# Layer 0 of a four-layer graph network: the transposes of a block's sums and of the next queries moved to the end of a round of scores

## The chip, the cores and the metric

The kernel runs on one core of a Trainium2 chip. The time is the device time of one execution in microseconds (us); the number to predict is the median over several executions. A profile of one further execution gives the busy time of each engine: PE (TensorE matmuls, with PEld for its weight loads), DVE (VectorE), ACT (ScalarE), POOL (GpSimd) and SP (SyncE, which here issues DMAs).

## The reference, cut to what matters

Four graph layers follow one another on x (4096 x 64) with one adjacency matrix adj (4096 x 4096, zeros and ones, about one entry in a thousand set). The change is in layer 0:

```python
h = jnp.maximum(_layernorm(x, axis=-1), 0.0)
h = lorentz_linear(h, W, b, scale)
q = lorentz_linear(h, Wq, bq, scale_q)
k = lorentz_linear(h, Wk, bk, scale_k)
att = 2.0 + 2.0 * (qm @ k.T)          # qm is q with its first column negated
att = adj * jax.nn.sigmoid(att / att_scale + att_bias)
support = att @ h
x = x + support / denorm              # a length of each row of support
```

Each layer begins with `_layernorm` and a maximum with zero. Layers 1 to 3 use the same adj: a weighted count over each row's last neighbours, a plain product, and a mean over neighbours.

## The kernel before, in words

**Tiling.** The 4096 rows whose sums are formed are cut into eight blocks of 512 (`NIB` blocks, numbered 7 down to 0, in this order). The 4096 rows that are summed over are cut into 32 tiles of 128, taken two at a time as a group g (`NG` = 16 groups). One step of layer 0 is one pair (block, g): `scores` (L910) makes two fp32 matmuls, each with half of PE's rows, into a PSUM tile `ps` of 128 x 1024; `sigmoids` (L926) applies the sigmoid on ACT, into `ps` itself or, for the first step of a round of four, into an SBUF tile `att`; `masked` (L932) multiplies by the mask on DVE into `att` (L940); `gather` (L942) multiplies `att` with the rows `fb` on PE and adds into the block's accumulator `acc`, each of its two matmuls in half of PE's columns (L947). Three `ps` tiles are used in turn: a score needs the tile of three scores before. The one of a round's first score is free when its sigmoid is done, the others when DVE's product is.

**Rounds.** The main loop (L1047) takes steps in rounds, of four as a rule, and in the first block of the loop (block 6) in rounds of 4, 4, 3 and 3. A round issues its scores one after the other and then the products of the round before. Each engine works through its own queue in the order in which the program emits the instructions. Before the loop, a planned part (`first_rows_and_block`) has done block 7 and two steps of block 6.

**Work between the rounds.** After each step of a round, `on()` (L1037) advances two things by one turn. `step()` advances a list of generators, each of which runs to its next `yield`; a job pushed with a number lets the jobs behind it go on only after that many turns. `rows0` (L878) is such a job, pushed when a block's accumulator is full: transposes of the block's sums (`turned`, L231, 128 x 128, four of them, into the PSUM tile `pt`), a copy of them on ACT (L237), an addition on POOL (L239), a square on ACT (L888), the sums `inn` on DVE (L891 to L894), an inverse square root (`rsqrt`: a first value on DVE, L256, then twelve small POOL instructions, L260 to L263), two POOL instructions of 256 elements (L896, L897), then `norm` for layer 1: `st` on DVE (L271), `xc` on POOL (L275), a square on ACT (L278), `va` on DVE (L281), a second `rsqrt` on POOL, `xc` on DVE (L297), and `split` (L245 on POOL, L248 on DVE). The second thing is `queries` (L870): two transposes of the next block's queries (L855, into the PSUM tile `pq`), and four copies of them on ACT into `qt` (L865). `pt` and `pq` share one PSUM buffer.

**What else is in the stage.** Every step issues one mask load on POOL's queue as long as there are any left (L175). From block 5 on, five steps of eight do a `check` (L342): a load of 256 KB on SP's queue and one DVE instruction on it (L356), which looks for entries of adj that are neither zero nor one. `count_constants` (L819) is a job of its own, in block 6, with POOL and DVE instructions. After layer 0, `chunks_counted` (L1139) runs 256 matmuls over the masks, with `step()` now and then, and the layer 1 products follow.

Before the change the transposes come where the generators' own counts of `yield` put them: those of `pt` two turns after `rows0` is begun, and those of `pq` six turns after `queries`.

Of the kernel before, what the change touches and what calls it, by code (L numbers as in the profile page):

```python
# [48 lines left out]
def kernel(  # L49
# [77 lines left out]
    def bc(col, r):  # L127

        return col.unsqueeze(2).to_broadcast([P, r, D])

    def over_rows(v, r):
        return v.unsqueeze(1).to_broadcast([P, r, v.shape[-1]])

    def model(general):
# [4 lines left out]
        def pool(name, bufs, on=stack, **kw):  # L139
            return on.enter_context(tc.tile_pool(name=name + sfx, bufs=bufs, **kw))  # L140
# [9 lines left out]
        def rows_in(gr):  # L150
# [10 lines left out]
        todo = [  # L161
            (ib, g) for ib in order0 for g in (first_cols if ib == order0[0] else range(NG))
        ]
        masks = {}

        def get_mask(mp, ib):

            masks[ib] = mp.tile([P, NT, IB], FP8, name=f"mask{ib}{sfx}")
# [30 lines left out]
        def rows_tile(name, tag, on=epi, bufs=1, dtype=F32):  # L199
            return on.tile([P, CI, D], dtype, tag=name, name=f"{name}{tag}{sfx}", bufs=bufs)  # L200

        def small(name, tag, on=epi, n=CI):
            return on.tile([P, n], F32, tag=name, name=f"{name}{tag}{sfx}")
# [14 lines left out]
        def turned(asb, b, tag, adding=False):  # L218


            shape = (P, CI, D if adding else P)
            if b is None:
                pt = pm.tile(list(shape), F32, tag="pr", name=f"pt{tag}{sfx}")
            else:
                pt = bank(b, f"pt{tag}", shape)
            for c in range(CI):
                part = asb[:, c * P : (c + 1) * P]
                if adding:
                    nc.tensor.matmul(pt[:, c, :], part, fold, start=True, stop=True)
                else:  # L230
                    nc.tensor.transpose(pt[:, c, :], part, ident)  # L231
            return pt

        def halves_added(to, asb, pt):

            v = asb.rearrange("p (c i) -> p c i", c=CI)
            nc.scalar.copy(v, pt)  # L237
            yield
            nc.gpsimd.tensor_tensor(to, v[:, :, 0:D], v[:, :, D:P], ALU.add)  # L239
            yield  # L240

        def split(h, s2, rows):


            nc.gpsimd.tensor_scalar(s2[:, rows, 0, :], h, 1.0 / STEP, None, ALU.mult)  # L245
            yield
            yield
            nc.vector.scalar_tensor_tensor(  # L248
                s2[:, rows, 1, :], s2[:, rows, 0, :], -STEP, h, ALU.mult, ALU.add
            )  # L250

        def rsqrt(v, tag, on=epi, n=CI, key=""):


            y, a = (small(f"rs_{a}{key}", tag, on, n) for a in "ya")
            nc.vector.tensor_scalar(  # L256
                y.bitcast(I32), v.bitcast(I32), -0.5, 1597463007.0, ALU.mult, ALU.add
            )
            for _ in range(3):
                nc.gpsimd.tensor_tensor(a, y, y, ALU.mult)  # L260
                nc.gpsimd.tensor_tensor(a, a, v, ALU.mult)
                nc.gpsimd.tensor_scalar(a, a, -0.5, 1.5, ALU.mult, ALU.add)
                nc.gpsimd.tensor_tensor(y, y, a, ALU.mult)  # L263
            return y
# [38 lines left out]
        def push(job, lag):  # L303

            jobs.append([job, lag])
# [20 lines left out]
        def drain():  # L326
            while jobs:
                step()

        def block(ib):  # L330
            return slice(ib * CI, (ib + 1) * CI)
# [514 lines left out]

        stream0 = pool("stream0", 1, l0) if general else None
        spare, turn = [], [0]
        qts = {}

        def queries_turned(ib, pt):

            for k in range(CI // 2):
                c = ib * CI + 2 * k
                nc.tensor.transpose(  # L855
                    pt[:, k, :], q_sb[:, c : c + 2, :].rearrange("p c d -> p (c d)"), ident
                )

        def queries_laid(ib, pt):

            qt = work.tile([P, IB], F32, tag="qt", name=f"qt_{ib}{sfx}", bufs=2)
            to = qt.rearrange("p (k c i) -> p k c i", k=CI // 2, c=2)
            for c in range(2):
                for s in range(2):
                    nc.scalar.copy(  # L865
                        to[s * D : (s + 1) * D, :, c, :], pt[c * D : (c + 1) * D, 0 : CI // 2, :]
                    )
            qts[ib] = qt

        def queries(ib):  # L870
            for _ in range(6):
                yield
            pt = pm.tile([P, CI, P], F32, tag="pr", name=f"pq_{ib}{sfx}")
            queries_turned(ib, pt)
            yield
            queries_laid(ib, pt)

        def rows0(ib, asb):  # L878
            tag = f"0_{ib}"
            rows = block(ib)  # L880
            yield
            yield
            pt = turned(asb, None, tag)
            yield
            sup = rows_tile("sup", tag)
            yield from halves_added(sup, asb, pt)
            sq = rows_tile("sq", tag)
            nc.scalar.activation(sq, sup, AF.Square)  # L888
            yield
            inn = small("inn", tag)  # L890
            nc.vector.tensor_reduce(inn, sq, AX.X, ALU.add)  # L891
            nc.vector.scalar_tensor_tensor(inn, sq[:, :, 0], -2.0, inn, ALU.mult, ALU.add)
            nc.vector.scalar_tensor_tensor(inn, inn, -1.0, inn, ALU.mult, ALU.max)
            nc.vector.tensor_scalar(inn, inn, 1e-8, None, ALU.max)  # L894
            rs = rsqrt(inn, tag)
            nc.gpsimd.tensor_tensor(sup, sup, bc(rs, CI), ALU.mult)  # L896
            nc.gpsimd.tensor_tensor(x_sb[:, rows, :], x_sb[:, rows, :], sup, ALU.add)  # L897
            yield
            yield
            yield  # L900
            yield
            h = yield from norm(rows, None, tag, False)
            yield from split(h, s2a, rows)
            ready.setdefault(1, set()).add(ib)

            nc.gpsimd.tensor_tensor(
                x_sb[:, rows, :], x_sb[:, rows, :], over_rows(bias1, CI), ALU.add
            )
# [116 lines left out]
        with tc.manual_schedule():  # L1025
            acc, late = first_rows_and_block()
            push(rows0(order0[0], evacuated(order0[0], acc, 0)), 10)
            pro_stack.close()
            mp1 = pool("mask_b", 1, side="right")
            for ib in order0[EARLY:]:  # L1030
                get_mask(mp1, ib)
            spare.append(pool("pp1", 1, l0, space=PSUM))
            if not general:
                push(count_constants(), 1)
            asking = iter(())

            def on():  # L1037
                step()
                next(asking, None)

            sizes = [2] * 8 if general else [4] * 4
            first = [2] * 7 if general else [4, 4, 3, 3]
            sizes = first + (NIB - 2) * sizes + [0]
            k, done = NG + 2, NG
            for size in sizes:  # L1047
                now = []
                for ib, g in todo[k : k + size]:
                    ps = scores(ib, g)  # L1050

                    if size == 4 and not now:
                        att = frm = sigmoids(ps, att_tile(ib, g))
                    else:
                        frm, att = sigmoids(ps), att_tile(ib, g)
                    masked(ib, g, frm, att)
                    now.append((ib, g, att))
                    load_masks(1)
                    k += 1
                    if k > 2 * NG and k % 8 in (0, 2, 4, 5, 7):  # L1060
                        check()
                    on()
                for ib, g, att in late:
                    at = done % NG
                    if at == 0:
                        acc = pa0.tile([P, IB], F32, tag="pa", name=f"acc0_{ib}{sfx}")
                        if ib > 0:
                            asking = queries(ib - 1)
                    gather(acc, fb, g, att, at)
                    if at == NG - 1:  # L1070
                        push(rows0(ib, evacuated(ib, acc, 0)), 10)
                    done += 1
                late = now
            if len(checks) % 2:
                check()
            if general:
                drain()
# [440 lines left out]
    with tc.If(any_odd[0] > 0):  # L1518
        model(True)
# [49 lines left out]
```

## Time and profile before

| | |
|---|---|
| median of three executions | 605.93 us (605.20 to 606.10) |
| the profiled execution | 605.98 us, of which the span 604.2 us |
| PE busy | 563.6 us (93%), 3012 matmuls |
| DVE busy | 484.8 us (80%) |
| ACT busy | 335.6 us (56%) |
| POOL busy | 238.1 us (39%) |
| scores, L916 on PE | 512 matmuls, 127.5 us busy |
| products, L947 on PE | 512 matmuls, 117.6 us busy |
| granted clock of PE, mean | 0.99 |

The span runs from the first to the last instruction of the profile, and 1.8 us of the profiled execution lie around it. In the views below, a line of a timeline has the start in us from the span's start, the length of the run of instructions in us, the engine, the line of the program, the operation, what is written and read, the shape and the number of instructions; in brackets the engine's idle time ahead of it, and what ended it. A line of the chain that ended last has a start, a length and a piece of work. A line of the table by stretch has the stretch, its length, the busy time and number of instructions of PE, PEld, DVE, ACT and POOL in it, PE's granted clock, the mean busy share of the DMA engines and the GB/s. Ends of matmuls are modelled, so starts are the safer numbers.

### The profile page before, as it was taken

What the parts mean: (1) busy time and instruction counts of PE and PEld (TensorE: products, weight loads), DVE (VectorE), ACT (ScalarE), POOL (GpSimd) and SP (SyncE); (2) the same over time, 40 slices, a digit from 0 to 9 for tenths busy, and PEclk for the clock granted to TensorE, in tenths of its full rate; (3) what the DMA queues carried; (4) which work ended last, traced back from release to release, by engine and by line L of the source; (5) the groups of instructions that cost most, each with busy time, mean ns of one, the idle gap of its engine ahead of it and who ended that gap; (6) DMA issues with size and microseconds to landing.
All of it is one profiled execution on the core that took longest, in us unless ns stands there. A gap on an engine that the chain in (4) does not pass through costs nothing.

```text
span 604.2 us, 8998 instructions
## 1 busy us (share of the span) xinstructions
PE 563.6 (93%) x3012; PEld 235.5 (39%) x3012; DVE 484.8 (80%) x941; ACT 335.6 (56%) x541; POOL 238.1 (39%) x459
## 2 busy tenths in 40 slices
PE   0777999899999999899999999999998999999995
PEld 0563333233333333233343343343443545454553
DVE  5769766699999999799966878879888669987753
ACT  1557657667666666676626677767766013441221
POOL 8422401585767675754335400100010305452252
PEclk9996999999999999999999999999999999999999
DMA  9992932679999999992262555555455476445921
GB/s 139 143 105 23 101 30 18 61 100 158 151 161 158 151 157 162 139 149 88 71 247 102 168 183 168 160 193 165 157 199 181 151 267 208 151 164 186 316 91 41
DMA packets 43015, 87.02 MB, mean 144 GB/s; under 512 B 5136, under 2 KB 22032, under 8 KB 42960
## 3 DMA queue, kind: packets, MB, share of 16 engines
q1 hardware_dynamic: 23808, 68.40, 34.4%
q0 software_dynamic: 18720, 17.57, 31.1%
q10 hardware_dynamic: 432, 0.40, 0.3%
q8 instruction: 25, 0.41, 0.3%
q14 instruction: 30, 0.25, 0.1%
HBM read 135.63 MB, written 1.05 MB: 226 GB/s over the span
## 4 chain that ended last, share of the span: by engine, by line
PE 86%; DVE 4%; ACT 4%; issue 2%; POOL 2%; DMA 2%; ACTq 0%; DVEq 0%; POOLq 0%
PE acc L1321 18%; PE ps L916 18%; PE acc L947 17%; PE acc L1249 9%; PE cnt L1211 9%; PE cnt L1221 3%; PE many L1144 2%; PE pt L231 2%; PE ps_h L624 1%; DVE att L940 1%; PE pr L1124 1%; DMA vec<-vecs_dram 1%; PE ps_q L624 1%; PE pn L1398 1%; ACT tq L767 1%
## 5 line engine op out<-in xcount | busy, mean ns | idle before, releaser
L916 PE MATMUL ps<-qt,kt 64*128 64x512 f32 x512 | 127.5, 623 | 3.5 <-DVE att L940 3.4
L356 DVE SCALAR_TENSOR_TENSOR ckw<-ckw 128x1024 f32<-128x1024 f32 x98 | 124.9, 1283 | 5.9 <-DMA ckw<-adjt_dram 5.7
L947 PE MATMUL acc<-att,fb 128*64 128x512 f32 x512 | 117.6, 599 | 0.0
L1237 ACT ACTIVATE w<-cnt 128x512 int16<-128x512 f32 x176 | 93.1, 597 | 42.8 <-PE cnt L1221 42.5
L940 DVE TENSOR_TENSOR att<-ps,mask 128x1024 f32<-128x1024 f32 x84 | 101.1, 1219 | 9.8 <-ACT ps L929 8.9
L929 ACT ACTIVATE ps<-ps,att_c,att_a 128x1024 f32<-128x1024 f32 x84 | 95.7, 1173 | 10.0 <-PE ps L916 7.0
L929 ACT ACTIVATE att<-ps,att_c,att_a 128x1024 f32<-128x1024 f32 x44 | 52.5, 1204 | 56.1 <-PE ps L916 53.1
L175 POOL DMA_DIRECT2D mask<-adjt_dram x128 | 70.3, 563 | 21.3 <-DMA mask<-adjt_dram 19.1
L916 PEld LDWEIGHTS ps<-qt,kt 64*128 64x128 f32 x512 | 44.7, 188 | 76.1 <-DVE att L940 21.5
L1235 DVE TENSOR_SCALAR w<-cnt 128x512 int16<-128x512 f32 x80 | 53.7, 687 | 23.1 <-PE cnt L1221 22.7
L940 DVE TENSOR_TENSOR att<-att,mask 128x1024 f32<-128x1024 f32 x44 | 56.3, 1292 | 18.2 <-ACT att L929 17.6
L1211 PE MATMUL cnt<-mask,after 128*128 128x512 fp8e4 x256 | 66.3, 379 | 2.0 <-DVE w L1235 1.5
L1249 PE MATMUL acc<-w,s2a 128*128 128x512 bf16 x256 | 66.5, 381 | 0.1
L947 PEld LDWEIGHTS acc<-att,fb 128*64 128x64 f32 x512 | 33.6, 136 | 79.2 <-issue 75.4
L275 POOL TENSOR_TENSOR xc<-x_sb,st 128x256 f32<-128x256 f32 x24 | 19.1, 795 | 108.4 <-DVE st L272 54.9
L1321 PE MATMUL acc<-mask,s2a 128*128 128x512 fp8e4 x256 | 57.8, 379 | 0.0
L1321 PE MATMUL acc<-mask,s2b 128*128 128x512 fp8e4 x256 | 57.7, 379 | 0.0
L260 POOL TENSOR_TENSOR rs_a<-rs_y 128x4 f32<-128x4 f32 x48 | 16.8, 350 | 81.6 <-DVE rs_y L256 72.3
L356 DVE SCALAR_TENSOR_TENSOR ck<-ck 128x512 f32<-128x512 f32 x60 | 44.9, 749 | 0.3 <-DMA ck<-adjt_dram 0.3
L1211 PEld LDWEIGHTS <-after 128*128 128x128 bf16 x256 | 24.8, 99 | 30.9 <-issue 3.5
L1321 PEld LDWEIGHTS <-s2b 128*128 128x128 f16 x256 | 25.0, 98 | 27.6 <-issue 0.8
L1321 PEld LDWEIGHTS <-s2a 128*128 128x128 f16 x256 | 24.6, 98 | 27.3
(194 smaller groups left out, 582.4 us busy)
## 6 DMA issues: line engine op xcount, KB each, us to landing
ckw<-adjt_dram SPq DMA_DIRECT2D x98, 512.0 KB, 3.5
mask<-adjt_dram POOLq DMA_DIRECT2D x128, 128.0 KB, 9.0
ck<-adjt_dram SPq DMA_DIRECT2D x60, 256.0 KB, 5.1
x_sb<-x_dram SPq DMA_DIRECT2D x4, 256.0 KB, 7.8
out_dram<-y POOLq DMA_DIRECT2D x6, 128.0 KB, 2.2
out_dram<-y ACTq DMA_DIRECT2D x2, 128.0 KB, 2.2
w_sb<-wts_dram SPq DMA_DIRECT2D x2, 80.0 KB, 7.6
vec<-vecs_dram ACTq DMA_DIRECT2D x1, 130.5 KB, 6.3
```

What stands on the lines that cost most here:

```text
L175: nc.gpsimd.dma_start(out=masks[ib][:, g * CG : (g + 1) * CG, :], in_=adjt[ib, g])
L275: nc.gpsimd.tensor_tensor(xc, xr, bc(st, CI), ALU.add)
L356: nc.vector.scalar_tensor_tensor(at, at, 0.0, at, ALU.not_equal, ALU.not_equal, accum_out=odd[:, k : k + 1])
L916: nc.tensor.matmul(ps[:, c, :], kt[half, g, :], qts[ib][half, :], start=True, stop=True)
L929: nc.scalar.activation(to, ps, AF.Sigmoid, bias=att_c, scale=att_a)
L940: nc.vector.tensor_tensor(att, frm, mask, ALU.mult)
L947: nc.tensor.matmul(acc[c * D : (c + 1) * D, :], lhs[:, t, :], rhs[:, c, :], start=(at == 0), stop=(at == NG - 1), skip_group_check=True,)
L1211: nc.tensor.matmul(cnt, after, masks[ib][:, t, :], start=True, stop=True, skip_group_check=True)
L1235: nc.vector.tensor_scalar(w, cnt, 0.0, None, ALU.max)
L1237: nc.scalar.activation(w, cnt, AF.Relu)
L1249: nc.tensor.matmul(accs[ib], both(s2a, t), w, start=(t == NT - 1), stop=False, skip_group_check=True,)
L1321: nc.tensor.matmul(acc, both(s2, t), masks[ib][:, t, :], start=(t == 0), stop=(t == NT - 1), skip_group_check=True,)
```

## The change

A flag, `edge`, tells the generators whether the step just emitted is the last of its round of scores. `rows0` now waits at least one turn and then until the flag is set before it transposes; `queries` waits three turns and then until the flag is set. After the loop the flag is left set. The instructions themselves are the same; what follows the transposes in the two generators follows by as many turns as before.

```diff
+        edge = [False]
         qts = {}
@@ def queries(ib):
-            for _ in range(6):
+            for _ in range(3):
+                yield
+            while not edge[0]:
                 yield
             pt = pm.tile([P, CI, P], F32, tag="pr", name=f"pq_{ib}{sfx}")
             queries_turned(ib, pt)
@@ def rows0(ib, asb):
             yield
-            yield
+            while not edge[0]:
+                yield
             pt = turned(asb, None, tag)
@@ the main loop
-                for ib, g in todo[k : k + size]:
+                for n, (ib, g) in enumerate(todo[k : k + size]):
+                    edge[0] = n == size - 1
                     ps = scores(ib, g)
@@ after the main loop
                 late = now
+            edge[0] = True
             if len(checks) % 2:
```

In the order in which the changed program emits its instructions, the transposes of `pt` of blocks 7 to 1 stand after the round's last score, where they stood before it; those of `pq` of blocks 4 to 0 stand after the last score of a block's third round, where they stood before the last score of its fourth. The later steps of `rows0` stand one step later, and ACT's copies of the queries stand between the sigmoids 12 and 13 of an ordinary block, where they stood after sigmoid 15.

## The prediction

> **What bounds the kernel now.** I read the busy shares first (PE 93%, DVE 80%, ACT 56%, POOL 39%), then the chain that ended last (86% of it on PE), then the stage of the change: a table by block of layer 0, the timelines of the engines inside it, and the chain around the two places where PE stands still. A "block" below runs from one block's first `acc` product to the next one's; the six full ones and the last, shorter one are, with PE, PEld, DVE, ACT and POOL busy in each:
>
> ```profile
> 95.03:129.54 34.51, 32.64 (x144) 11.00 (x142) 26.32 (x46) 23.75 (x27) 18.28 (x48) 1.00 0.51 50
> 129.54:159.77 30.23, 30.23 (x136) 10.41 (x134) 28.47 (x50) 21.01 (x24) 18.11 (x42) 1.00 1.00 154
> 220.67:253.37 32.70, 31.11 (x136) 10.26 (x138) 28.81 (x49) 21.22 (x25) 21.24 (x48) 1.00 0.99 150
> 253.37:283.71 30.34, 30.34 (x136) 10.44 (x138) 28.84 (x49) 21.00 (x24) 16.88 (x38) 1.00 0.68 128
> ```
>
> To see: in an ordinary block PE has no idle time, but DVE has only 1.5 to 1.8 us of it. The two blocks left out are like the second (30.40 and 30.50). So PE sets the end, with DVE close behind. PE idles in the first block (1.87 us) and in one later one (1.59 us).
>
> The timeline of PE prices the thing that is moved:
>
> ```profile
> 104.11 2.85 PE L916 MATMUL ps<-qt,kt 64*128 64x512 f32 x12
> 106.89 0.44 PE L855 MATMUL pq<-ident,s2a 128*128 128x128 f32 x2
> 107.26 3.65 PE L947 MATMUL acc<-att,fb 128*64 128x512 f32 x16
> ...
> 155.35 2.85 PE L916 MATMUL ps<-qt,kt 64*128 64x512 f32 x12
> 158.13 0.66 PE L231 MATMUL pt<-ident,asb 128*128 128x128 f32 x4
> 158.71 1.13 PE L916 MATMUL ps<-qt,kt 64*128 64x512 f32 x4
> 159.77 3.65 PE L947 MATMUL acc<-att,fb 128*64 128x512 f32 x16
> 163.36 3.70 PE L916 MATMUL ps<-qt,kt 64*128 64x512 f32 x16
> 166.99 3.65 PE L947 MATMUL acc<-att,fb 128*64 128x512 f32 x16
> ```
>
> From start to start: four undivided scores take 166.99-163.36 = 3.63, four products 3.59. Three scores take 2.78, the 0.85 left for a further one being its pure length. But the fourth score behind the transposes takes 159.77-158.71 = 1.06. So a switch of the form of matmul costs about 0.2 us. The first query transposes of layer 0 happen to lie at the end of a round already (106.89): they take 0.37 us up to the products, as they do between scores (143.12 to 143.49), and the products behind them keep their 3.58. Moving transposes to the end of a round thus saves one switch of 0.2 us, with nothing paid for it on PE.
>
> **What the skill says.** The Trainium skill, TensorEngine Tiling (Array Packing), Key Properties: changing the tiling mode drains TensorE. The scores use half the rows, the products half the columns, the transposes all: the trace agrees, with 0.2 us. SBUF — State Buffer, Who interferes with whom: a DVE instruction with two SBUF inputs and a GpSimd instruction that reads SBUF block each other. The trace agrees: a 0.19 us step of `rsqrt` (L262) took 1.04 us at 158.01, under a mask product from SBUF. PSUM — Partial Sum Buffer, Engine vs sequencer instructions: the queues of ScalarE, VectorE and GpSimd are strictly in order; the trace shows ACT's square L278 holding up sigmoids that were ready (from 241.80 to 244.48, below).
>
> **The change on PE.** Twelve groups of transposes move from before a round's last score to behind it: the sums `pt` of blocks 7 to 1 (seven), and the queries `pq` of blocks 4 to 0 (five), which also go from the fourth round to the third. 12 x 0.20 = 2.4 us saved. `pq` of block 5 goes from one round's end to another's: nothing. `pt` of block 0 moves earlier inside the counting products L1144: nothing, as PE runs through there with or without it (0.58 us either way).
>
> **The change in the first block.** Its two holes, by the chain that ended last and PE's timeline:
>
> ```profile
> 113.12 0.36 ACT qt L865
> ...
> 114.66 1.19 ACT ps L929
> ...
> 115.87 1.22 DVE att L940
> ...
> 118.62 1.22 DVE att L940
> ...
> 119.90 1.99 PE L916 MATMUL ps<-qt,kt 64*128 64x512 f32 x8 [1.57 <-DVE att L940]
> ```
>
> The four query copies (1.51 us) sit between sigmoids 13 and 14, and everything behind them is late; three PSUM tiles take turns, so the third score of the next round waits for DVE's product 15. Now they sit behind sigmoid 10. By hand, from the start X of that round (before: 110.84): sigmoid 13 at +1.18, product 13 on DVE +2.39, `st` 0.55, product 14 at +4.08, the constants 1.61 us, product 15 from +6.83 to +8.05. The score needs it 0.26 earlier than its own start (0.06 to see it, 0.2 for weights), so it starts at +8.31; undisturbed it would at 2.78+2.73+0.2+1.71 = +7.42. The hole is 0.89, where before it is 1.57+0.2 = 1.77: 0.88 saved. The second hole (0.30 at 126.84, and the 0.2 to start again, and a little before it: 0.58) came from product 3, queued on DVE behind `xc` L297, which waited for POOL. That step is now behind product 3: 0.58 saved. Together 1.5 us.
>
> **What is late next.** Two new waits, in each ordinary block. The rows for them, of DVE, POOL and ACT, around the block start at 148.13:
>
> ```profile
> 140.63 0.17 DVE L256 TENSOR_SCALAR rs_y<-inn 128x4 int32<-128x4 int32 x1
> ...
> 147.20 2.73 POOL L175 DMA_DIRECT2D mask<-adjt_dram  x5
> 149.90 0.68 POOL L275 TENSOR_TENSOR xc<-x_sb,st 128x256 f32<-128x256 f32 x1
> ...
> 145.89 1.52 ACT L865 COPY qt<-pq 64x256 f32<-64x256 f32 x4
> ...
> 150.61 0.42 ACT L278 ACTIVATE sq<-xc 128x256 f32<-128x256 f32 x1
> ```
>
> (a) The query copies, today after sigmoid 15 where ACT is idle, come between sigmoids 12 and 13. From the start of that round: sigmoid 12 at +1.17, the copies +2.28 to +3.80, sigmoid 13 ends +4.97, product 13 on DVE +5.01, product 14 +6.15, a check 0.61, product 15 from +7.90 to +9.12. The next block's scores start at 3.63+3.59 = +7.22 (no transposes in this round now), its third score at +9.13, and needs +9.38. Late by 0.25; with the checks at their mean (0.75, not 0.68 us) 0.3. Five blocks: 1.5 us. What shrinks the round is itself what uncovers this: today it has 0.57 more.
>
> (b) `inn`, the sum of squares, moves behind product 11 and a check: it ends about 9.7 us after its round starts (2.41 to the first product, four of 1.14, `split`'s 0.37, two checks of 0.61, its own 1.15), where before it was 140.80-133.12 = 7.7. From there to `xc` takes POOL 149.90-140.80 = 9.1 us: twelve steps of `rsqrt`, two of 256 elements, and five mask DMAs of 0.55 that are issued in between. So `xc` starts at 18.8, and the next block at 7.59+7.22 = 14.8: `xc` is 4.0 into it (before 1.8). ACT's square then starts at +4.7 and holds back sigmoid 2, queued behind it, to +5.05, with its end +6.22; product 2 on DVE +6.26, `va` 0.76, product 3 +8.16 to +9.38. Round two's third score would start at +9.38 and needs +9.64: late by 0.26. The mean check instead of the short one, three times, makes it 0.45; with POOL's steps blocked once more by a product from SBUF (0.85) it is up to 1.3; with POOL less blocked than before, nothing. I take 0.45. It meets four blocks, since in the last one no mask is left to issue: 1.8 us.
>
> No DMA changes in number; the mask issues keep their places between POOL's other work but for one that goes ahead of the first `halves_added`, and SP's order is the same. The checks' loads follow the checks. Behind layer 0 nothing is due: block 0's normed rows are wanted only by the last products of the first counting group.
>
> **Sum.** -2.4 -1.5 +1.5 +1.8 = -0.6 us. Against the profiled execution, 605.98 us with a span of 604.2: 605.4, span 603.6. The median is 605.93, so 605.3. A difference of 0.2% (1.2 us) is about what a measurement of this kernel can tell from none.
>
> **Rivals.** (1) Full gain: the two waits stay covered, because POOL is blocked less in the place where its steps now run (one check less beside them), and (a) is absorbed: -2.4-1.5 = -3.9, 602.0 us. For it: PE alone would allow 29.8 us a block; against it: (a) needs only rows that don't vary. 0.2. (2) Slower: wait (b) feeds on itself. A late `xc` delays ACT, that delays DVE, whose products then meet POOL's steps, and the next `inn` is later again. DVE has 28.5 us of work in a block that would shrink to 29.8. Its place is ACT's square before sigmoid 2, its price the 0.85 of a blocked step: 0.45+0.85 = 1.3 a block, 3.4 us in all more than forecast, 608.7; from 0.6 a block on the change gains nothing, from 0.9 it is slower by 0.2%. A middle value of 1.0 gives 607.5. 0.2. (3) The one disturbance of the stage goes elsewhere: POOL idles 2.07 us at 238.67, with no semaphore behind it, just before it issues five masks, and block 2 loses 2.1 us through the same square. Should it fall where nothing waits for POOL: 605.3-2.1 = 603.2. The order of POOL's work around it is unchanged, so 0.1. That the edit does nothing is out: the emitted order of PE, ACT and DVE shows the moves.
>
> **Chances and range.** The forecast has 0.5, with a range of its own from 603.9 to 606.5 (wait (b) between nothing and 0.75). Faster by over 0.2% (below 604.7): rivals 1 and 3, and a fifth of the forecast, 0.38. Slower (above 607.1): most of rival 2, with a sliver of the forecast, 0.2. Between, 0.42. The range that leaves out no more than 2 in 10 is 602.3 to 607.2.
>
> **What would show it.** Right: undivided rounds of 3.63 on PE with `pt` at 0.58 and `pq` at 0.37 behind them; a hole of under 1 us, not 1.6, in the first block and none at 126; the third scores of the first two rounds of a block waiting for DVE by some tenths; ACT's square 4 to 5 us into a block, waiting for POOL. Blocks near 30.5. Wrong: blocks of 29.8 to 30.0 (no waits), or above 31 (rival 2); transposes at a round's end costing PE more than 0.37 and 0.58; or a change of time behind 305 us.

## The result, and the profile after

The changed kernel is slower: 609.0 us (median of six executions, 608.1 to 610.3) against 606.0 us for the kernel before on the same chip; the ratio is 1.0060, with a 95% interval of 1.0046 to 1.0073. The forecast was 605.3 us with a range up to 607.2.

Two profiled executions, 605.98 us before and 608.21 us after, are best compared by stages, cut at landmarks on PE: the first score, the matmul `pw` behind the last product of layer 0, the first `cnt` of the counting stage (layer 1), the first product of layer 2.

| stage, us | before | after | difference |
|---|---|---|---|
| up to the first score | 54.65 | 52.57 | -2.1 |
| layer 0, first score to `pw` | 251.20 | 249.96 | -1.2 |
| `many`, from `pw` on (L1144, now L1151) | 14.99 | 14.99 | 0 |
| counting stage | 146.66 | 152.24 | **+5.6** |
| layers 2 and 3 | 136.74 | 136.72 | 0 |

The first row is not the change's: its instructions stand as before, and over thirteen profiled executions of this study it took between 52.5 and 54.9 us. It also scatters the medians; where a microsecond matters below, I read the stage and not the whole. Layer 0 won 1.2 us. The loss lies in a stage that the forecast had put at nothing.

PE's timeline at the start of the counting stage, after (start, length, engine, line, operation, shape, count, idle time ahead and what ended it):

```profile
321.07 0.59 PE L1218 MATMUL cnt<-mask,after 128*128 128x512 fp8e4 x2
325.43 0.59 PE L1218 MATMUL cnt<-mask,after 128*128 128x512 fp8e4 x2 [3.77 <-DVE w L1242]
```

PE stands still for 3.77 us (such a stand of PE is called a hole below), and what it waits for is a `w` of DVE: until DVE (or ACT) has turned a `cnt` into a `w`, its PSUM bank is not free for the next `cnt`. DVE at the same time, after:

```profile
318.16 0.69 DVE L1242 TENSOR_SCALAR w<-cnt 128x512 int16<-128x512 f32 x1
323.83 0.94 DVE L248 SCALAR_TENSOR_TENSOR s2a<-s2a,xc 128x256 f16<-128x256 f16 x1 [4.98 <-POOL s2a L245]
324.69 1.27 DVE L1242 TENSOR_SCALAR w<-cnt 128x512 int16<-128x512 f32 x2
```

Between the first `w` and the next two stands the second half of `split` of block 1, L248, which has nothing to do with them. It waits 4.98 us for its first half on POOL, L245, and everything behind it in DVE's queue waits too. POOL, after:

```profile
318.20 0.20 POOL L260 TENSOR_TENSOR rs_a<-rs_y 128x4 f32<-128x4 f32 x1 [1.85 <-DVE rs_y L256]
...
322.26 0.72 POOL L902 TENSOR_TENSOR x_sb<-x_sb,sup 128x256 f32<-128x256 f32 x1
322.95 0.85 POOL L245 TENSOR_SCALAR s2a<-xc 128x256 f16<-128x256 f32 x1
```

L245's input (`xc` of block 1, L297 on DVE) is ready at 316.6. But on POOL's queue L245 now stands behind all of block 0's `rsqrt` (318.20 to 321.49) and the two larger instructions after it. The same places before, on POOL and on DVE:

```profile
319.24 1.68 POOL L245 TENSOR_SCALAR s2a<-xc 128x256 f16<-128x256 f32 x1 [0.44 <-DVE xc L297]
321.50 0.23 POOL L260 TENSOR_TENSOR rs_a<-rs_y 128x4 f32<-128x4 f32 x1 [0.58 <-DVE rs_y L256]
```

```profile
321.26 0.42 DVE L248 SCALAR_TENSOR_TENSOR s2a<-s2a,xc 128x256 f16<-128x256 f16 x1
321.60 0.68 DVE L1235 TENSOR_SCALAR w<-cnt 128x512 int16<-128x512 f32 x1
```

There L245 went ahead of block 0's `rsqrt`, and L248 ahead of the first `w`. The change turned both orders round: with the flag left set after the loop, block 0's transposes come after 36 matmuls of `many` and no longer after some 68, while block 1's chain of instructions runs one step later than before.

The hole has a tail. The table by stretch, after (stretch, its length, busy time of PE, PEld, DVE, ACT and POOL, then PE's granted clock, DMA share, GB/s):

```profile
326.00:328.00 2.00, 2.00 (x14) 0.81 (x14) 1.06 (x3) 1.57 (x3) 0.61 (x1) 0.65 0.00 0
328.00:330.00 2.00, 2.00 (x8) 0.41 (x6) 0.00 (x0) 0.62 (x2) 0.00 (x0) 0.50 0.00 0
```

In the four microseconds behind the hole PE is busy throughout, but at 0.65 and 0.50 of its clock; from 330 on it is 1.00 again. What it didn't do there is 2.00 x (0.35 + 0.50) = 1.7 us. Hole and slow stretch together are 5.5 of the stage's 5.6 us.

In layer 0 the table by block answers to the one of before:

```profile
92.94:125.71 32.77, 32.17 (x144) 11.21 (x143) 26.14 (x46) 23.49 (x27) 16.97 (x45) 1.00 0.51 50
125.71:156.08 30.37, 30.31 (x136) 10.52 (x135) 28.24 (x50) 21.30 (x25) 18.67 (x40) 1.00 0.97 150
156.08:187.03 30.95, 30.33 (x136) 10.52 (x135) 28.28 (x49) 21.37 (x26) 21.23 (x47) 1.00 1.02 157
217.99:248.94 30.95, 30.32 (x135) 10.52 (x134) 28.24 (x49) 21.10 (x25) 21.25 (x47) 1.00 1.00 154
```

The first block is 1.74 us shorter than before, the one with POOL's disturbance (the last line) 1.75, and the others are up to 0.6 longer. The two waits that the forecast named are there, in the two rounds of PE around the line between two blocks, after:

```profile
174.47 3.93 PE L921 MATMUL ps<-qt,kt 64*128 64x512 f32 x16
...
181.91 1.99 PE L921 MATMUL ps<-qt,kt 64*128 64x512 f32 x8
184.52 1.99 PE L921 MATMUL ps<-qt,kt 64*128 64x512 f32 x8 [0.62 <-DVE att L945]
186.44 0.66 PE L231 MATMUL pt<-ident,asb 128*128 128x128 f32 x4
```

From start to start, the first round takes 178.33-174.47 = 3.86 us and the second 186.44-181.91 = 4.53, where an undisturbed one takes 3.63.

### The profile page after: what moved, and what is told of

It reads as the page before. It is cut to its first block, busy times and chain, and to the rows that moved or that the text cites. A ratio compares the mean times of both kernels' runs of the same rounds, so it can differ in the third digit from the quotient of the medians.

```text
span 606.5 us, 8998 instructions
## 1 busy us (share of the span) xinstructions
PE 560.6 (92%) x3012; PEld 234.4 (39%) x3012; DVE 483.6 (80%) x941; ACT 335.2 (55%) x541; POOL 238.9 (39%) x459
## 3 DMA queue, kind: packets, MB, share of 16 engines
HBM read 135.63 MB, written 1.05 MB: 225 GB/s over the span
## 4 chain that ended last, share of the span: by engine, by line
PE 66%; DVE 11%; POOL 9%; issue 5%; ACT 5%; DMA 4%; SPq 0%; ACTq 0%; POOLq 0%; DVEq 0%
PE acc L1328 14%; PE ps L921 12%; PE acc L952 12%; PE acc L1256 9%; PE cnt L1218 9%; DVE att L945 4%; PE cnt L1228 3%; DMA ckw<-adjt_dram 2%; DVE ckw L356 1%; PE pt L231 1%; POOL mask L175 1%; POOL rs_a L260 1%; DMA mask<-adjt_dram 1%; ACT ps L934 1%; PE ps_h L624 1%
## 5 line engine op out<-in xcount | busy, mean ns | idle before, releaser
L921 PE MATMUL ps<-qt,kt 64*128 64x512 f32 x512 | 125.1, 618 | 2.7 <-DVE att L945 2.5
L934 ACT ACTIVATE att<-ps,att_c,att_a 128x1024 f32<-128x1024 f32 x44 | 52.5, 1204 | 57.4 <-PE ps L921 54.4
L175 POOL DMA_DIRECT2D mask<-adjt_dram x128 | 70.1, 558 | 21.3 <-DMA mask<-adjt_dram 19.8
L275 POOL TENSOR_TENSOR xc<-x_sb,st 128x256 f32<-128x256 f32 x24 | 20.0, 831 | 112.9 <-DVE st L272 74.3
L356 DVE SCALAR_TENSOR_TENSOR ck<-ck 128x512 f32<-128x512 f32 x60 | 43.1, 718 | 0.0
```

Of the source, the lines that this page charges most:

```text
L175: nc.gpsimd.dma_start(out=masks[ib][:, g * CG : (g + 1) * CG, :], in_=adjt[ib, g])
L356: nc.vector.scalar_tensor_tensor(at, at, 0.0, at, ALU.not_equal, ALU.not_equal, accum_out=odd[:, k : k + 1])
L921: nc.tensor.matmul(ps[:, c, :], kt[half, g, :], qts[ib][half, :], start=True, stop=True)
L934: nc.scalar.activation(to, ps, AF.Sigmoid, bias=att_c, scale=att_a)
```

## The experiments

All eleven kernels are small edits of the two. Ratios are to the kernel before, run on the same chip, with 95% intervals; the last two columns are stages of the profiled execution, to be held against 251.20 and 146.66 us before, 249.96 and 152.24 after. Theory Q, formed from the trace after: a queue of the counting stage makes the loss. Theory L, its rival: the loss comes from layer 0's waits, or from PE's clock by itself.

| kernel | median, us | ratio | layer 0 | counting stage |
|---|---|---|---|---|
| e1_block0_old | 603.63 | 0.9969 (0.9953 to 0.9984) | 249.91 | 146.62 |
| e2_second_half_later | 603.27 | 0.9956 (0.9941 to 0.9971) | 249.99 | 146.71 |
| e3_tail_alone | 612.37 | 1.0101 (1.0066 to 1.0136) | 251.73 | 153.55 |
| e4_square_later | 602.90 | 0.9940 (0.9918 to 0.9963) | 248.47 | 146.73 |
| e5_copies_later | 606.45 | 1.0032 (1.0020 to 1.0044) | 251.91 | 146.47 |
| e6_both_later | 600.88 | 0.9937 (0.9920 to 0.9953) | 246.40 | 146.57 |
| e7_st_only_waits | 604.44 | 0.9990 (0.9980 to 0.9999) | 249.95 | 147.08 |
| e8_both_and_old_tail | 599.81 | 0.9923 (0.9907 to 0.9940) | 246.23 | 146.47 |
| e9_best | 599.18 | 0.9899 (0.9882 to 0.9915) | 245.33 | 146.58 |
| e10_queries_alone | 604.77 | 0.9998 (0.9986 to 1.0009) | 251.53 | 146.49 |
| e11_rows_alone | 610.63 | 1.0079 (1.0057 to 1.0101) | 252.57 | 150.44 |

**Block 0's transposes where they were.** On the changed kernel:

```diff
             rows = block(ib)
             yield
-            while not edge[0]:
+            if ib == 0:
+                yield
+            while ib > 0 and not edge[0]:
                 yield
             pt = turned(asb, None, tag)
```

> The changed kernel, but block 0's sums are transposed after two steps as before, so that POOL's first half of block 1's split (L245) stands ahead of block 0's rsqrt chain again. Theory Q (a queue of the counting stage: DVE's second half L248 of block 1 waits for POOL and holds the next w): the 3.77 us hole near the start of the counting stage and the slow clock behind it are gone, the stage from the first cnt to the first layer-2 product takes 146.7 us instead of 152.2, and the time is 609.0-5.6 = 603.4 us. Theory L (the loss comes from layer 0's own waits or from the clock by itself): the stage stays within 1 us of 152.2 and the time at 608 to 610.

Measured 603.63 us. The counting stage is back at 146.62, the clock stays at 1.00, and the changed kernel with this one part undone is faster than the kernel before. Layer 0 is as in the changed kernel, to 0.05 us. So layer 0's waits are not where the loss is, and the slow clock goes with the hole. Its POOL and its DVE:

```profile
317.75 0.85 POOL L245 TENSOR_SCALAR s2a<-xc 128x256 f16<-128x256 f32 x1 [0.44 <-DVE xc L297]
```

```profile
319.52 0.41 DVE L248 SCALAR_TENSOR_TENSOR s2a<-s2a,xc 128x256 f16<-128x256 f16 x1
```

POOL has its old order again (block 0's `rsqrt` follows at 319.16), but DVE keeps the changed kernel's, with L248 behind the first `w` of 318.92. There it waits for nothing. Of the two orders that the change turned round, DVE's costs nothing by itself; the one that counts is POOL's.

**Which engine's queue.** Here POOL's order stays the changed kernel's, and on DVE L248 of block 1 and `st` of block 0, with what follows `st`, go behind five `w`:

```diff
-        def split(h, s2, rows):
+        def split(h, s2, rows, later_half=0):
             nc.gpsimd.tensor_scalar(s2[:, rows, 0, :], h, 1.0 / STEP, None, ALU.mult)
-            yield
-            yield
+            for _ in range(2 + later_half):
+                yield
@@ rows0: 6 turns instead of 4 ahead of norm for block 0, and
-            yield from split(h, s2a, rows)
+            yield from split(h, s2a, rows, 3 if ib == 1 else 0)
```

> The changed kernel, but DVE's second half of block 1's split comes three steps later and block 0's row sums (st) two steps later, both behind five w of the counting stage; POOL's order is the changed kernel's. Theory Q, in the form that it is DVE's queue that stops PE: the hole is gone though POOL is as late as in the changed kernel, the clock stays near 1, 603.4 us (602.9 to 604.2). Theory P (PE itself waits for what POOL makes late, through the rows or a buffer): the hole stays at 3 us or more and the time at 608 to 610.

Measured 603.27 us, the stage 146.71. Its POOL and its DVE:

```profile
324.90 0.85 POOL L245 TENSOR_SCALAR s2a<-xc 128x256 f16<-128x256 f32 x1
```

```profile
322.21 1.29 DVE L1240 TENSOR_SCALAR w<-cnt 128x512 int16<-128x512 f32 x2 [1.47 <-PE cnt L1226]
327.24 0.42 DVE L248 SCALAR_TENSOR_TENSOR s2a<-s2a,xc 128x256 f16<-128x256 f16 x1
```

L245 is as late as in the changed kernel (5.5 us behind the first `cnt`, 5.4 there), and costs nothing: the `w` now wait for PE, not PE for them. A late POOL was harmless; a DVE instruction queued ahead of urgent ones and waiting for it was not.

**The tail alone.** On the kernel before, only the sums of blocks 1 and 0 move to the end of a round:

```diff
             rows = block(ib)
             yield
-            yield
+            if ib > 1:
+                yield
+            while ib < 2 and not edge[0]:
+                yield
             pt = turned(asb, None, tag)
```

> The kernel before, with only the sums of blocks 1 and 0 transposed at the end of a round's scores; all other blocks and all queries as before. Theory Q: the hole alone, 605.9+5.6-0.2 = 611.3 us, with layer 0 as before (251.3 us from the first score to pw). Theory L: 605.7 us.

Measured 612.37 us, a ratio of 1.0101: the loss in full, with layer 0 nearly as before (251.73). The hole is 4.02 us, the stage 6.9 us longer; the clock stays slow for longer here (0.68, 0.50, 0.50, 0.61 in four stretches of 2 us). Together the three runs settle the cause: it can be taken away at either of two places, POOL's order or the place of L248 on DVE, and put into the old kernel by itself.

**Wait (b): the square one score later.** On the kernel of the first run, from here to e6; in blocks 7 to 2 only:

```diff
             nc.gpsimd.tensor_tensor(xc, xr, bc(st, CI), ALU.add)
             yield
+            for _ in range(later_square):
+                yield
             sq = rows_tile("sq", tag)
```

> The kernel of the first run, with ACT's square of the norm (L278) one score later in blocks 7 to 2, so that it stands behind sigmoid 2 and not before it. If wait (b) is this square (forecast 0.45 a block, the trace of the changed kernel shows about 0.9 in three blocks): the holes of 0.62 us in the second rounds are gone, and the time is 603.4-2.7 = 600.7 us. If what POOL makes late is only handed on to the next instruction (va on DVE, or sigmoid 3), at most 1 us is won: 602.4 or above.

Layer 0 became 1.4 us shorter than in the first run (248.47 against 249.91); 2.7 were expected. The holes of 0.62 us in the second rounds are gone, so the square was their cause. But the first rounds, 3.86 us in the first run, take 4.30 in four blocks, with a hole that the first run doesn't show. PE of this kernel:

```profile
179.06 1.99 PE L925 MATMUL ps<-qt,kt 64*128 64x512 f32 x8 [0.41 <-DVE att L949]
```

**Wait (a): the copies three scores later**, behind sigmoid 15:

```diff
             queries_turned(ib, pt)
-            yield
+            for _ in range(4):
+                yield
             queries_laid(ib, pt)
```

> The kernel of the first run, with the copies of the queries (transposed at the end of the third round) three scores later, behind sigmoid 15 as before the change. If wait (a) is these copies between sigmoids 12 and 13: the first rounds of a block take 3.63 us instead of 3.86, five times 0.25, 602.3 us; the second rounds keep their 4.53. If DVE is full anyway and hands its lateness on: first rounds unchanged, 603.4 us.

This expectation missed. The first rounds are down to 3.63 us, as expected, so the copies between sigmoids 12 and 13 are wait (a). But layer 0 is 2.0 us *longer* than in the first run. Its block 6 has its old hole of 1.57 back (0.60 before this edit), and the second rounds grew, three of them from 4.53 to 5.15. PE, and ACT's square:

```profile
185.92 1.13 PE L924 MATMUL ps<-qt,kt 64*128 64x512 f32 x4 [0.21 <-DVE att L948]
187.81 1.99 PE L924 MATMUL ps<-qt,kt 64*128 64x512 f32 x8 [0.77 <-DVE att L948]
```

```profile
183.12 0.42 ACT L278 ACTIVATE sq<-xc 128x256 f32<-128x256 f32 x1 [2.28 <-POOL xc L275]
```

The square now waits 2.28 us for POOL; in the changed kernel it is 1.89. That the second wait grows by more (0.62 us in three blocks) than the first gave up (0.22) can be read from the two traces. PE comes to the second round 0.22 earlier, and `xc` (L275) starts 5.05 us into the block, where it was 4.65 in the first run. These 0.40 arise on POOL, in the chain ahead of `xc`: one step of `rsqrt` (L262) takes 0.55 us and not 0.19 and the last addition (L905) 1.23 and not 0.73, each while DVE runs a check, and the instruction between them (L904) 0.61 and not 1.05 (in the first run the last two are L904 and L903).

**Both later.**

> Both: the square one score later and the copies three scores later. The square alone moved the wait from the second rounds into the first ones (4.30 instead of 3.86). If that rest is the copies' (sigmoid 13 and so product 13 late), all rounds are undivided at 3.63, the full blocks near 29.8 us, layer 0 about 2.5 us shorter than with the square alone: 600.2 us. If it is DVE's own work, which fills a block: blocks stay near 30.4 and the time at 602 or above.

Layer 0 is 246.40 us, 3.5 less than in the first run, and an ordinary block:

```profile
187.39:217.22 29.83, 29.83 (x135) 10.69 (x134) 28.31 (x49) 21.07 (x25) 21.07 (x47) 1.00 1.04 158
```

No round waits from block 5 on, and DVE has its 28.3 us of work all the same: it isn't DVE's amount of work that made the waits, but the two places in ACT's order. Singly the two edits gave -1.4 and +2.0, together -3.5. Measured by medians, 600.88 us on a chip where the kernel before took 604.85; the ratio 0.9937 is as good as that of the square alone (0.9940), since the starts of the executions scatter by as much as is at stake. The gain shows in layer 0, 246.40 against 248.47 us with the square alone, and again in the two kernels below that build on this one (246.23 and 245.33).

**A shorter stand in the same queue.** The changed kernel with `later_half` for block 1 as in the second run, but block 0's `st` left between the third and the fourth `w`.

> The changed kernel with DVE's second half of block 1's split three steps later, but block 0's row sums (st) left between the third and the fourth w of the counting stage, where they wait for POOL's sum of x_sb. By theory Q the same kind of hole, only shorter: st can start at 323.0 in the changed kernel's times, the fourth w is due at 321.6, some 0.6 are buffered: a hole of 1 to 2 us, and 603.4+1.3 = 604.7 us. If the slow clock comes behind any such hole, up to 1.8 us more: 606.5. If st stops nothing: 603.3.

The stand is there (DVE's `st` waits 1.49 us for POOL), but PE's hole is only 0.45 us, the stage 0.4 longer, and the clock stays at 1.00. The kind of hole is as expected, its size isn't: I put the fourth `w` 0.9 us too early. In the second run it comes 2.17 us behind the second one; here it comes 3.32 behind, so it is 1.15 late, of which the buffers cover 0.7.

**The old tail for blocks 1 and 0**, on top of both:

```diff
-            if ib == 0:
+            if ib < 2:
                 yield
-            while ib > 0 and not edge[0]:
+            while ib > 1 and not edge[0]:
                 yield
```

> Both later, and the sums of blocks 1 and 0 transposed after two steps as before the change, so that the end of layer 0 and the counting stage have the old order. Against the run with both later: pw waits about 0.7 us instead of 1.7 for ACT's last copy (a gain of 1.0), one more switch of form costs 0.2: 599.4 us, if that run gives 600.2. If the last wait is not set by block 1's chain: 600.4.

Measured 599.81 us. `pw` waits 0.69 us for ACT's last copy, not the 1.53 with both later; one switch and a small hole near the end of layer 0 (0.21) come back, and layer 0 is 0.2 us shorter, layer 0 and counting stage together 0.3. So the wait at the end of layer 0 is block 1's chain, as expected, but worth little in the sum.

**A version that beats both.** On the last kernel, block 6's copies of the queries stay behind sigmoid 10, where the change put them (one turn and not four, for the queries of block 5 alone).

> The last run's kernel (square and copies later, old tail), but block 6's copies stay behind sigmoid 10, where the change puts them. The one hole left in layer 0, 1.65 us in block 6, becomes the changed kernel's 0.60: 1.0 us less than the last run, a ratio of 0.9906 to the kernel before. If block 6's hole is set by something else than the copies: 0.9923 again.

599.18 us, a ratio of 0.9899 (0.9882 to 0.9915): 1% faster than the kernel before. Block 6's hole is 0.75, not 1.65, and layer 0 takes 245.33 us, 5.9 less than before.

**Each part of the change alone**, on the kernel before: only the edit in `queries`, then only the one in `rows0`.

> The kernel before with the queries' part of the change alone. By the sum of the trace: five switches of form -1.0, block 6's first hole -0.9, wait (a) +1.25 at most, the counting stage as before (146.7): -0.6 us, a ratio of 0.999. If the stall of the counting stage came from the queries' part: +5, a ratio of 1.008.

> The kernel before with the rows' part of the change alone (blocks 7 to 0). Seven switches -1.4, block 6's second hole -0.6, POOL's 2.07 us stand in block 2 moved away -2.1, wait (b) +2 (less than 3.2, as the fourth round still has the transposes of the queries in it), the wait at the end of layer 0 +1.0, the counting stage +5.6: +4.5 us, a ratio of 1.0075. If the loss needs both parts: 1.000 or below.

The queries alone: ratio 0.9998, the counting stage untouched, layer 0 at +0.3 where -0.6 was expected. Wait (a) is the miss: the first rounds take 2.51+1.91 = 4.42 us instead of 3.63, since in the old order `st` (0.55 us) still stands ahead of product 15 on DVE. The rows alone: ratio 1.0079, as expected in the sum, with its parts otherwise: layer 0 at +1.4 (second rounds of 4.95, wait (b) 1.3 us in three blocks and 0.9 in one), `many` and the counting stage together +5.5. The sums of layer 0 don't add up either: +0.3 and +1.4 alone, -1.2 together. Each part relieves a wait of the other's: with the rows moved `st` goes behind product 15, and with the queries moved wait (b) is 0.9 us and not 1.3.

## Why the prediction was wrong, by its own steps

**The step that failed** is the last one under "What is late next", that behind layer 0 nothing is due, with its companion, that block 0's earlier `pt` costs nothing "as PE runs through there with or without it". Both look at PE and at who wants block 0's *rows*. True as far as it goes: the transposes take 0.59 us either way, and the late rows hurt nobody (second run). What was not asked is what block 0's POOL instructions now stand ahead of: L245 of block 1, with L248 behind it on DVE, and the `w` behind L248. The emitted order of POOL and DVE showed it: L245 after block 0's `rsqrt`, L248 between two `w`. The wait could be estimated from the trace before, too: twelve steps of 0.28 and two of 0.7 us are 4.8 us of POOL, and L245 itself takes 0.85. DVE's L248 waited 4.98, as its wait began 0.65 after the first of these steps. With the slow clock behind the hole (1.7 us), which no step had foreseen, it is worth +5.6 us, and turns the forecast's -0.6 into +5.0. The forecast's list of signs of being wrong ends with this one: "a change of time behind 305 us".

**The switch of form**, 0.2 us: right. With the waits gone a block takes 29.83 us, and 30.23 before: two switches, 0.40.

**Block 6**: right. The round with the hole (0.60 idle) takes 4.51 us, 0.88 more than an undisturbed one (forecast 0.89, which counts the time to start again), the second hole is gone, and the block is 1.74 shorter, against 1.5 and a switch.

```profile
116.84 1.99 PE L921 MATMUL ps<-qt,kt 64*128 64x512 f32 x8 [0.60 <-DVE att L945]
```

**Wait (a)**: right in place and size, 0.23 us in four blocks and 0.33 in one, 1.25 in all against 1.5. But the size holds only together with the rows' part.

**Wait (b)**: right in its mechanism and too small. Second rounds of 3.84, 4.53, 4.53, 4.53 and 3.91 us make 3.2 us above 3.63; the forecast was 1.8, with 0.45 each. The term mis-sized is the chain ahead of `inn`. The prediction put 0.37 us for L248 ahead of it; DVE's timeline, after:

```profile
163.27 0.94 DVE L248 SCALAR_TENSOR_TENSOR s2a<-s2a,xc 128x256 f16<-128x256 f16 x1
```

```profile
162.76 1.17 POOL L239 TENSOR_TENSOR sup<-asb 128x256 f32<-128x256 f32 x1
```

All six L248 of blocks 7 to 2 take 0.41 before; in the changed kernel the five after the first take 0.94 or 0.95. The POOL instruction beside them is L239, which adds the halves of the next block's sums. Before, where the two met, they began together (164.98 and 164.99), and L248 took 0.41 and L239 0.99; now L239 is there 0.51 us ahead and L248 takes the longer time. With the square later L239 no longer runs beside L248, which is back at 0.42. The Trainium skill (SBUF — State Buffer, Who interferes with whom) describes this case: a DVE instruction with two inputs in SBUF contends with a GpSimd instruction that reads SBUF. The 9.1 us from `inn` to `xc` were right: 9.2. So `xc` came 4.67 us into the next block's scores and not 4.0. The forecast's upper bound for one wait, 1.3, would have held it.

Rival 2 had the direction, more than 0.45 a block, but only part of the mechanism. The first wait is 0.21 us and the three after it 0.90, all alike, so it grows once and then no further; and the 0.5 us are lost on DVE's L248, not on a step of POOL. The price that rival 2 names, a step of POOL held up beside DVE, is in the run with the copies later: 0.40 us a block.

**Rival 3**, at 0.1: it happened. POOL's stand of 2.07 us ahead of five masks is gone from that place, and a mask of 227.74 has 1.40 us ahead of it, where POOL has nothing to do until 232. It goes with the order of the instructions, not with one execution: of the kernels here with the rows of layer 0 as before, all have it (2.07 and 2.08 us in the two new ones); with the rows moved, none has. The prediction kept the odds low because "the order of POOL's work around it is unchanged". It had itself noted the one mask issue that changes places. What makes POOL stand there these runs don't show.

**The sum.** For layer 0: -2.4 (switches), -1.5 (block 6), +1.25 (a), +3.2 (b), -2.1 (POOL's stand), and +1.0 at the end, where ACT's last copy stands behind block 1's square and `pw` waits 1.72 instead of 0.69, which no step had foreseen: -0.55, measured -1.2. Most of the rest can come from this: (a) and (b) are counted from rounds without any wait, while three blocks of before took together 0.55 more than the shortest. That layer 0 came out so near its forecast of -0.6 is in part luck: the larger wait (b) (+1.4) and the wait ahead of `pw` (+1.0) were missed, and POOL's stand (-2.1), which had a chance of 0.1, made up for most of it. Then +5.6 in the counting stage. The whole is +4.3 by the stages, within the +2.8 to +4.4 us of the interval.

## What to carry to other kernels

When a chain of small steps is moved in time, go through the queue of every engine it uses to its very end, past the stage of the change, and ask of each instruction that changes places with another one not only who wants its result, but what stands behind it and what stands behind those who wait for it. A wait of an in-order queue costs what is queued behind it, so a cheap cure, which worked here for L248 and for the square with the copies, is to issue the waiting instruction later. And two covered waits of one loop are not additive: one of two edits was worth -1.4, the other +2.0, both -3.5, so undo or try them together before dropping either.

## What the runs showed of the hardware

PE's clock drops behind some stands: it is below 1.00 in two stretches of 2 us in the changed kernel, in four in the one with the tail alone. The Trainium skill (TensorE: Matmul & The Clock Gate, Part 1: The HAM clock gate) states half clock after an idle window of some 3.4 us. The stands of 3.77 and 4.02 us agree. But the clock also fell behind shorter ones, so by these runs 3.4 us is no safe bound. It did so in the kernel with the rows alone: behind 2.26 us in the counting stage, and behind the 1.72 us ahead of `pw`, its table by stretch:

```profile
306.00:308.00 2.00, 1.96 (x22) 1.03 (x26) 1.35 (x7) 0.00 (x0) 0.00 (x0) 0.67 1.01 401
308.00:310.00 2.00, 2.00 (x24) 0.52 (x14) 1.78 (x3) 0.00 (x0) 0.00 (x0) 0.50 0.68 231
```

`many` took 16.66 us there instead of 14.99. The same stand of 1.72 us ahead of `pw` was followed by full clock in five other kernels, the changed one among them, and so were the holes of 1.57 and 1.65 us in block 6. When a stand of that length brings the slow clock and when not, these runs don't tell; it was not tried. In that kernel the 1.7 us lost in `many` were mostly won back at the hole behind it, which was 2.26 us instead of 3.77: counted from `pw`, POOL had its L245 ready as early as in the changed kernel (21.4 and 21.3 us), while the first `cnt` came 1.7 us later.
